# An attention kernel with top-1 experts: the row sum carried inside the probability tiles, one buffer of projection weights, and two router comparisons that read PSUM

## The chip, the cores and the metric

The kernel runs on one core of a Trainium2 chip. The metric is the device time of one execution in microseconds. Five engines work side by side, each through its own queue in order: TensorE (PE; PEld is its weight load), VectorE (DVE), ScalarE (ACT), GpSimd (POOL) and SyncE (SP), which here only issues DMAs. They wait for each other through semaphores. PE writes to PSUM, eight banks of 128 x 512 floats; DVE and ACT read it.

## The reference

Inputs are x of 4 x 2048 x 512 floats and the weights. The layer norm is without weights. Attention has 16 heads of 32, and filters queries and keys by a mask of their frequencies; the experts see the first 100 tokens that chose each of them.

```python
xn = layernorm(x)
q, k, v = split(xn @ w_qkv)                       # 16 heads of 32
q, k = spectral_filter(q), spectral_filter(k)     # rfft, times sigmoid(mask), irfft
attn = softmax(q @ k.T / sqrt(32))
y = (attn @ v) @ w_out + b_out

probs = softmax(xn @ w_gate)                      # 8 experts
best = argmax(probs)                              # the first one at equal values
# place of the token among those of its expert (cumsum); kept when it is below 100
expert = (dispatched @ w_expert + b_expert) * gate
x = x + y + expert
```

All of it is in float32.

## The kernel before

The work is cut into 16 **groups** k (four batches times four groups of four heads), each into four **blocks** n of 512 queries, each into eight **windows** w of two key tiles (128 keys each, one called even and one odd). There are 512 windows. Per tile and pair of heads u, PE adds a bias (the negative row maximum, negm, as three bf16 rows, `shift`) and the scores (`scores`) into two PSUM banks; ACT takes the exponential into a probability tile of 128 x 2 x 2 x 512 floats (8 KB per partition); one tile later PE multiplies it with the values (`products`), and DVE adds the result to `num` (ACT copies the first one into it).

The maxima of a later block are computed in the same windows: PE computes the scores once more the other way round (`max_matmuls`, array<-q,k and array<-k,q in the profile), DVE reduces them (`max_reduce`, part<-array). Two banks that lie side by side are reduced by one instruction, banks 7 and 0 by two (`joined`). `max_close` (line 468) turns the maxima of a block: PE transposes, ACT copies (rest<-array), POOL splits them into three bf16 rows (row<-rest), SP stores these to negm. It runs at the end of a block's seventh window (window 6), and the next block needs it with its first matmul.

**The row sum.** The softmax's denominator is the sum of all 16 tiles of a block. In the window after a pair, POOL issues a DMA that adds the odd tile to the even one (`pair`, line 823, even<-odd in the profile). One window later POOL adds this to the block's own tile `acc`, in two halves (`add_to`, line 826, acc<-acc,even). Tile 0 of a block is `acc` itself. Buffers: `acc` two, even three, odd two (lines 156 to 167). A buffer is free again when every reader of it is done.

**Closing a block.** `close_steps` (line 621) gives steps with a distance in windows from the block's end: `fold` (2) sums `acc` over the keys on PE and stores the sums (sums<-den), `fetch` (3) loads them spread over all partitions (few<-sums), `invert` (4) takes reciprocals on DVE and stores them (inverse<-few), `spread` (5) loads them as factor, `divide` (6) multiplies on POOL (ot<-num,factor), `result` (7, 7, 8, 8) projects a quarter each on PE and copies it to y on ACT, `add` (9) adds y to the output by a POOL DMA (out_dram<-y). The last block of all closes in `close_last` (line 666), with four tiles left to PE.

**Order.** Inside the main loop every compute instruction stays in the order of the program on its engine. The order between these works is an agenda, a list of steps for each window: half of a window's steps run after the even tile, half after the odd one. `plan` (line 774) fills it: the 12 projections of group k + 1 (`query_key`, `value`, with weights wg), the loading of weights (`load_qkv_weights`, line 374), in every third group of a batch the statistics and the bias of the next batch (x loaded to xs, POOL adds b_out, xs stored to the output), in every fourth its normalization, transposes and routing. SP's DMAs are placed by the scheduler, which may issue them earlier than the program says as long as their data are there. `place_experts` (line 756) puts the experts into the last groups.

**Routing** (lines 294 to 317) works on tiles of 128 x 16 x 8: the best probability per token (`best`), a comparison with it, a weight that falls with the expert's number (`ranked`), and a second comparison (`first_best`) which leaves one expert per token. Both comparisons are DVE instructions with two inputs in SBUF.

In the profile nearly all of this has line L82, the helper that keeps the order; it is told apart by tiles.

Of the kernel before, what the change touches and what calls it, by code (L numbers as in the profile page):

```python
# [101 lines left out]
def attention_and_top1_experts(ctx: ExitStack, tc: tile.TileContext, a: dict, out: bass.AP):  # L102
# [52 lines left out]
    chunks = ctx.enter_context(tc.tile_pool(name="chunks", bufs=2))  # L155
    probs_pool = ctx.enter_context(tc.tile_pool(name="probs", bufs=2))
    work = ctx.enter_context(tc.tile_pool(name="work", bufs=2))
# [6 lines left out]
    def probs(odd):  # L164

        name = "odd" if odd else "even"
        return probs_pool.tile([P, 2, 2, QB], F32, tag=name, name=name, bufs=2 if odd else 3)

# [43 lines left out]
    def token_stage(b):  # L212
# [81 lines left out]
        def wide(row):  # L294
            return row.unsqueeze(2).to_broadcast(full)


        def below_top():
# [9 lines left out]
        def best():  # L308
            on.vector.reduce_max(gate, probs, axis=AX.X)
            on.vector.tensor_tensor(chosen, probs, wide(gate), ALU.is_equal)  # L310

# [3 lines left out]
        def first_best():  # L315
            on.vector.reduce_max(first, chosen, axis=AX.X)
            on.vector.tensor_tensor(chosen, chosen, wide(first), ALU.is_equal)

# [55 lines left out]
    def load_qkv_weights(k):  # L374
        wg[k] = weights.tile([P, NR, 3, P], F32, name="wg")
        nc.sync.dma_start(out=wg[k], in_=wd[k % NG])
# [244 lines left out]
    def close_steps(k, n, num, acc):  # L621
# [29 lines left out]
        def divide():  # L651
            held["ot"] = work.tile([P, QB], F32, tag="ot", name="ot")
            on.gpsimd.tensor_tensor(held["ot"], num, held["factor"], ALU.mult)
# [8 lines left out]

        steps = [(2, fold), (3, fetch), (4, invert), (5, spread), (6, divide)]
        return steps + [(7, result, 0), (7, result, 1), (8, result, 2), (8, result, 3), (9, add)]

    def close_last(k, n, num, tiles, y):

        b = k // NG
        pf = row_sums(tiles)
        ot = work.tile([P, QB], F32, tag="ot", name="ot")  # L670
        den = work.tile([P, QB], F32, tag="den", name="den", bufs=1)
        for t in range(TQ):
            cols = slice(t * P, (t + 1) * P)
            on.vector.reciprocal(den[:, cols], pf[:, cols])
            on.gpsimd.tensor_tensor(ot[:, cols], num[:, cols], den[:, cols], ALU.mult)
        for t in range(TQ):
            on.vector.tensor_tensor(y[:, t, :], y[:, t, :], project(k, ot, t), ALU.add)
            if t % 2 == 1:
                nc.sync.dma_start(out=o[b, n, :, t - 1 : t + 1, :], in_=y[:, t - 1 : t + 1, :])
# [39 lines left out]
    for i, item in enumerate(stream[:MAX_AHEAD]):  # L719
# [14 lines left out]
        if i in closing:  # L734
            max_close(*closing[i])
    load_qkv_weights(1)

# [4 lines left out]
    def at(window, step, *args):  # L742
        agenda[window].append(lambda: step(*args))
# [12 lines left out]
    def place_experts(start):  # L756


        begin, fetch, measure, scale, expert = expert_steps()
        first = start + 18  # L760
        at(first, begin)
        for i in range(ST):
            at(first + 1 + i, fetch, i)
            at(first + 3 + i, measure, i)
        at(first + 11, scale)
        for i in range(ST + 2):
            at(first + 12 + i, expert, i)
        for i in range(ST):
            free = start + GW + i * NW + 10
            for step in (gather_row, add_row, scatter_row):  # L770
                at(free, step, i)
                free += 1

    def plan(k):
# [18 lines left out]
        if k + 2 < B * NG:  # L793
            at(start + GW // 2, load_qkv_weights, k + 2)
        first, last = len(first_projections) if k == 0 else 0, GW - 1
        if c == NG - 2 and b + 1 < B:
# [11 lines left out]
        elif c == NG - 1:  # L808
# [7 lines left out]
            for i in range(len(first_route)):  # L816
                at(start + 10 + i, follow_route, i)
            first, last = 10, GW
        steps = projections(k + 1)
# [5 lines left out]

    def add_to(acc, tile):
        for u in range(2):
            on.gpsimd.tensor_tensor(acc[:, u], acc[:, u], tile[:, u], ALU.add)

# [4 lines left out]
    for k in range(B * NG):  # L834
        plan(k)
        for n in range(NQ):
            num = work.tile([P, QB], F32, tag="num", name="num")
            acc = probs_pool.tile([P, 2, 2, QB], F32, tag="acc", name="acc")
            tiles = {0: acc}
            for w in range(NW):  # L840
# [7 lines left out]
                for j in (even, odd):  # L848
                    if j > 0:
                        tiles[j] = probs(j == odd)  # L850
                    for u in range(2):
# [22 lines left out]
                if not last or w < NW - 1:  # L874
                    pairs[window + 1] = tiles[even], tiles[odd]
                    if 0 < w and not (last and w == NW - 2):
                        adds[window + 2] = acc, tiles[even]
                if last and w == NW - 2:
# [3 lines left out]
            if not last:  # L882
                for after, *step in close_steps(k, n, num, acc):
                    at(window + after, *step)
    products(*left)
    for step in agenda[window]:
        step()
    close_last(k, n, num, [acc, *(tiles[j] for j in (NT - 4, NT - 2, NT - 1))], y)
    for steps in agenda[window + 1 :]:
# [35 lines left out]
```

## Time and profile before

| | |
|---|---|
| Median of 3 runs | 4593.77 us (4593.59 to 4596.07) |
| The profiled execution | 4593.43 us, its span 4591.6 us |
| Granted PE clock | 0.99 |
| Busy PE, DVE, ACT, POOL | 4422.1, 3121.1, 2592.4, 2998.8 us |
| POOL adds to the row sum (128 x 1024) | 892, 2541 ns each |
| Exponentials (128 x 512) | 4096, 603 ns each |
| DMAs that add odd to even | 511, 1024 KB, 7.9 us to landing (447 of them; 7.5 for the 64 into acc) |
| DMAs that add y to the output | 63, 1024 KB, 9.7 us to landing |
| wg loads | 16, 768 KB |
| DMA queue of POOL (q0) | 606.88 MB, 67.1% of the 16 DMA engines |

How to read it: *busy* is the time in which an engine had an instruction, as a share of the span. *Idle before* a group of instructions is the time that its engine stood still just in front of them, and the releaser is what ended it. The *chain* goes back from the last instruction, at each step to what released it or to the instruction before it on its engine, so its shares add up to the span. The *clock* is the share of full speed that PE was granted. Times in a timeline are us from the start of the span.

### The profile page before, as it was taken

Reading aid. Unit: us, or ns where it says so; the run is one execution under the profiler, and the core shown is the slowest. Engines: PE = TensorE matmul, PEld = TensorE weight load, DVE = VectorE, ACT = ScalarE, POOL = GpSimd, SP = SyncE. Lnnn points to the kernel's source line nnn. Section 1 sums busy time; section 2 is a strip of 40 time slices with the busy share of each in tenths; the row PEclk is TensorE's granted clock in tenths of the full one; section 3 lists DMA queues with packets and bytes.
Section 4 is the critical chain, followed back from the end, with each engine's and each line's share of the span. In section 5 each row is a group of like instructions: output and inputs, shape, how many; then the busy total and the mean of one; then the engine's idle time right before and its main releaser. Section 6 shows DMA issues by size and latency. Waiting matters only on the chain.

```text
span 4591.6 us, 106112 instructions
## 1 busy us (share of the span) xinstructions
PE 4422.1 (96%) x44438; PEld 1879.6 (41%) x44438; DVE 3121.1 (68%) x3605; ACT 2592.4 (56%) x4937; POOL 2998.8 (65%) x2081
## 2 busy tenths in 40 slices
PE   6999999999999999999999999999999999999997
PEld 3434343433434344344343434344444444434332
DVE  4667677775666777776567676777667776677772
ACT  3445555565555555557455555555655565555564
POOL 0458666765676667677477666667567774776766
PEclk9999999999999999999999999999999999999998
DMA  4567787786676877788667777878767775777787
GB/s 124 135 145 143 149 160 150 174 195 150 133 154 140 165 147 152 149 194 196 132 133 155 152 154 142 163 153 210 164 123 159 150 160 118 153 164 160 154 170 151
DMA packets 193233, 708.89 MB, mean 154 GB/s; under 512 B 47778, under 2 KB 54084, under 8 KB 127344
## 3 DMA queue, kind: packets, MB, share of 16 engines
q0 software_dynamic: 110576, 606.88, 67.1%
q1 hardware_dynamic: 77800, 91.56, 6.4%
q8 instruction: 348, 5.70, 0.5%
q10 hardware_dynamic: 4376, 3.67, 0.4%
q14 instruction: 133, 1.09, 0.1%
HBM read 77.09 MB, written 89.99 MB: 36 GB/s over the span
## 4 chain that ended last, share of the span: by engine, by line
PE 78%; DMA 10%; POOL 5%; issue 3%; ACT 2%; DVE 1%; SPq 0%; ACTq 0%; POOLq 0%; DVEq 0%
PE array L82 78%; DMA even<-odd 6%; POOL acc L82 4%; DMA inverse<-few 1%; DMA factor<-inverse 1%; ACT odd L82 1%; DMA sums<-den 1%; ACT even L82 1%; DVE part L82 1%; DMA negm<-row 0%; SPq L647 0%; POOL ot L82 0%; DMA wd<-in_L_attn_w_qkv_dram 0%; DMA few<-sums 0%; PE array L387 0%
## 5 line engine op out<-in xcount | busy, mean ns | idle before, releaser
L82 DVE TENSOR_REDUCE part<-array 128x2 f32<-128x1024 f32 (+1 forms) x2292 | 2433.2, 1106 | 1258.8 <-PE array L82 1247.0
L82 POOL TENSOR_TENSOR acc<-acc,even 128x1024 f32<-128x1024 f32 x892 | 2167.8, 2541 | 333.9 <-DMA even<-odd 332.7
L82 PE MATMUL array<-k,q 32*128 32x512 f32 x8192 | 2219.0, 622 | 10.7 <-issue 7.1
L82 PE MATMUL array<-q,k 32*128 32x512 f32 x8192 | 2051.9, 594 | 1.7 <-issue 1.7
L82 ACT ACTIVATE odd<-array 128x512 f32<-128x512 f32 x2048 | 1059.7, 603 | 485.9 <-issue 228.6
L82 ACT ACTIVATE even<-array 128x512 f32<-128x512 f32 x1792 | 931.9, 603 | 454.9 <-PE array L82 361.1
L82 POOL DMA_DIRECT2D even<-odd x447 | 412.4, 923 | 820.3 <-ACT odd L82 706.0
L82 PEld LDWEIGHTS array<-k,q 32*128 32x128 f32 x8192 | 808.7, 184 | 180.3 <-DVE num L82 71.6
L82 PE MATMUL array<-negm,ones_b 3*128 3x512 bf16 x4096 | 797.8, 382 | 25.0 <-DMA negm<-row 9.1
L82 PEld LDWEIGHTS array<-q,k 32*128 32x128 f32 x8192 | 751.5, 186 | 22.0 <-issue 13.3
L82 DVE TENSOR_TENSOR num<-num,array 128x512 f32<-128x512 f32 x960 | 651.6, 679 | 110.9 <-PE array L82 70.8
L82 PEld LDWEIGHTS <-ones_b 3*128 3x128 bf16 x4096 | 203.5, 92 | 914.4 <-issue 781.9
L82 PE MATMUL array<-odd,v 128*32 128x512 f32 x4096 | 548.0, 606 | 26.4 <-ACT even L82 25.8
L82 PE MATMUL array<-even,v 128*32 128x512 f32 x3584 | 483.5, 611 | 32.3 <-ACT odd L82 32.0
L82 PE MATMUL array<-xnT,wg 128*32 128x512 f32 x4032 | 464.0, 592 | 1.0 <-DVE part L82 1.0
L82 PE MATMUL array<-wo,ot 128*32 128x512 f32 x2048 | 259.0, 598 | 21.5 <-POOL ot L82 12.1
L82 PEld LDWEIGHTS array<-xnT,wg 128*32 128x32 f32 x4032 | 132.0, 110 | 303.1 <-issue 269.7
L82 PEld LDWEIGHTS array<-odd,v 128*32 128x32 f32 x4096 | 81.2, 108 | 421.2 <-ACT even L82 363.5
L82 PEld LDWEIGHTS array<-wg,xnT 128*32 128x32 f32 x8192 | 226.1, 110 | 39.5 <-issue 21.3
L82 PE MATMUL array<-wg,xnT 128*32 128x128 f32 x8192 | 235.8, 273 | 1.2 <-issue 1.2
L82 ACT COPY y<-array 128x512 f32<-128x512 f32 x252 | 147.7, 586 | 142.8 <-PE array L82 142.8
L82 PEld LDWEIGHTS array<-even,v 128*32 128x32 f32 x3584 | 71.2, 108 | 377.4 <-ACT odd L82 366.2
(144 smaller groups left out, 1715.3 us busy)
## 6 DMA issues: line engine op xcount, KB each, us to landing
even<-odd POOLq DMA_DIRECT2D x447, 1024.0 KB, 7.9
acc<-odd POOLq DMA_DIRECT2D x64, 1024.0 KB, 7.5
out_dram<-y POOLq DMA_DIRECT2D x63, 1024.0 KB, 9.7
xs<-in_L_attn_x_dram SPq DMA_DIRECT2D x31, 1024.0 KB
out_dram<-xs SPq DMA_DIRECT2D x16, 1024.0 KB
factor<-inverse SPq DMA_DIRECT2D x252, 64.0 KB
wg<-wd SPq DMA_DIRECT2D x16, 768.0 KB
wo<-in_L_attn_w_out_dram SPq DMA_DIRECT2D x16, 256.0 KB
```

The lines of the kernel that those rows point to most:

```text
L82: done = act(*args, **kwargs)
```

## The change

The block's own tile goes. Every key tile lies in an even or odd tile, and POOL adds the sum of the pair before to the pair's even tile, so the last even tile of a block holds the sum. There are five even and three odd buffers. wg has one buffer, and its load stands at a group's last window in the program (for group 1 after the first group's own projections); the projections of groups 0 and 3 of a batch shift by a window or two. `divide`, `result` and `add` of a block stand one window later each, and so do the experts' steps behind them; ot has one buffer. In the last close the sum of all pairs up to the sixth lies in tile NT - 6. In the router, ACT copies the operand of both comparisons into a PSUM bank, and DVE reads it there.

```diff
-        return probs_pool.tile([P, 2, 2, QB], F32, tag=name, name=name, bufs=2 if odd else 3)
+        return probs_pool.tile([P, 2, 2, QB], F32, tag=name, name=name, bufs=3 if odd else 5)
...
+        def in_array(of):
+
+            copy = bank()[:, 0 : NT * E].rearrange("p (i e) -> p i e", e=E)
+            on.scalar.copy(copy, of)
+            return copy
...
-            on.vector.tensor_tensor(chosen, probs, wide(gate), ALU.is_equal)
+            on.vector.tensor_tensor(chosen, in_array(probs), wide(gate), ALU.is_equal)
...
-            on.vector.tensor_tensor(chosen, chosen, wide(first), ALU.is_equal)
+            on.vector.tensor_tensor(chosen, in_array(chosen), wide(first), ALU.is_equal)
...
-        wg[k] = weights.tile([P, NR, 3, P], F32, name="wg")
+        wg[k] = weights.tile([P, NR, 3, P], F32, name="wg", bufs=1)
...
-            held["ot"] = work.tile([P, QB], F32, tag="ot", name="ot")
+            held["ot"] = work.tile([P, QB], F32, tag="ot", name="ot", bufs=1)
...
-        steps = [(2, fold), (3, fetch), (4, invert), (5, spread), (6, divide)]
-        return steps + [(7, result, 0), (7, result, 1), (8, result, 2), (8, result, 3), (9, add)]
+        steps = [(2, fold), (3, fetch), (4, invert), (5, spread), (7, divide)]
+        return steps + [(8, result, 0), (8, result, 1), (9, result, 2), (9, result, 3), (10, add)]
...
-    load_qkv_weights(1)
...
-            free = start + GW + i * NW + 10
+            free = start + GW + i * NW + 11
...
-            at(start + GW // 2, load_qkv_weights, k + 2)
-        first, last = len(first_projections) if k == 0 else 0, GW - 1
+            at(start + GW - 1, load_qkv_weights, k + 2)
+        if k == 0:
+            at(len(first_projections), load_qkv_weights, 1)
+        first, last = len(first_projections) + 2 if k == 0 else 0, GW - 1
...
-            first, last = 10, GW
+            first, last = 10, GW - 1
...
-    def add_to(acc, tile):
+    def add_to(tile, sum_before):
         for u in range(2):
-            on.gpsimd.tensor_tensor(acc[:, u], acc[:, u], tile[:, u], ALU.add)
+            on.gpsimd.tensor_tensor(tile[:, u], tile[:, u], sum_before[:, u], ALU.add)
...
-            acc = probs_pool.tile([P, 2, 2, QB], F32, tag="acc", name="acc")
-            tiles = {0: acc}
+            tiles = {}
...
-                    if j > 0:
-                        tiles[j] = probs(j == odd)
+                    tiles[j] = probs(j == odd)
...
-                        adds[window + 2] = acc, tiles[even]
+                        adds[window + 2] = tiles[even], tiles[even - WIN]
...
-                for after, *step in close_steps(k, n, num, acc):
+                for after, *step in close_steps(k, n, num, tiles[NT - WIN]):
...
-    close_last(k, n, num, [acc, *(tiles[j] for j in (NT - 4, NT - 2, NT - 1))], y)
+    close_last(k, n, num, [tiles[j] for j in (NT - 6, NT - 4, NT - 2, NT - 1)], y)
```

More of the change, by code (lines that the diff above doesn't have):

```diff
@@ L155, in attention_and_top1_experts @@
     chunks = ctx.enter_context(tc.tile_pool(name="chunks", bufs=2))
-    probs_pool = ctx.enter_context(tc.tile_pool(name="probs", bufs=2))
+    probs_pool = ctx.enter_context(tc.tile_pool(name="probs", bufs=3))
     work = ctx.enter_context(tc.tile_pool(name="work", bufs=2))
@@ L669, in close_last @@
         pf = row_sums(tiles)
-        ot = work.tile([P, QB], F32, tag="ot", name="ot")
+        ot = work.tile([P, QB], F32, tag="factor", name="ot", bufs=1)
         den = work.tile([P, QB], F32, tag="den", name="den", bufs=1)
```

## The prediction

> **What bounds the kernel now.** I read the page first. TensorE (PE) is busy nearly all the time, and PE is most of the chain that ended last; a tenth of the chain is DMA and a twentieth GpSimd (POOL).
>
> ```profile
> PE 4422.1 (96%) x44438; PEld 1879.6 (41%) x44438; DVE 3121.1 (68%) x3605; ACT 2592.4 (56%) x4937; POOL 2998.8 (65%) x2081
> ...
> PE 78%; DMA 10%; POOL 5%; issue 3%; ACT 2%; DVE 1%; SPq 0%; ACTq 0%; POOLq 0%; DVEq 0%
> ```
>
> A busy PE is not PE at its peak, so I looked for the loss in durations. I cut the span at the first bias matmul (array<-negm,ones_b) of each head group and asked for the stretches. Groups 1, 2, 4, 5, 6, 8, 9, 10, 12 and 14 do the same PE work (x2732 to x2736 matmul records). Shown are groups 6, 8, 14 and the last, 15 (columns: length, busy of PE, PEld, DVE, ACT, POOL, then PE clock, DMA share, GB/s).
>
> ```profile
> 1818.90:2099.60 280.70, 266.33 (x2732) 111.08 (x2728) 200.89 (x243) 158.02 (x300) 200.04 (x138) 0.99 0.82 178
> ...
> 2400.40:2663.70 263.30, 261.89 (x2732) 110.82 (x2728) 188.99 (x213) 154.38 (x296) 183.47 (x126) 1.00 0.76 152
> ...
> 4063.10:4325.60 262.50, 261.77 (x2732) 110.95 (x2728) 189.10 (x210) 154.38 (x296) 189.57 (x130) 1.00 0.78 157
> 4325.60:4591.60 266.00, 225.87 (x1890) 83.52 (x1886) 150.26 (x173) 147.84 (x286) 178.06 (x118) 0.94 0.80 162
> ```
>
> The reader is to see that equal work takes 262.5 in one group and 280.7 in another. Against group 14 the other nine lose 5.2, 18.3, 8.4, 1.7, 18.2, 0.8, 7.0, 12.3 and 3.5 us: 75.4 in all. The largest losses are where POOL and DMA have most to do (groups 2, 6 and 10, which load the next batch). Groups 3, 7, 11 and 13 have other PE work; against group 11, groups 3 and 7 lose 10.4 more.
>
> The list of waits names the causes (us in total, times, longest), and one passage of the chain in group 6 shows how a pair's DMA reaches PE:
>
> ```profile
> ACT even L82 <- POOL acc L82: 83.9, 45, 2.7
> ...
> POOL ot L82 <- DMA factor<-inverse: 64.4, 25, 4.7
> ...
> ACT odd L82 <- DMA even<-odd: 48.3, 17, 8.2
> ...
> PEld array L82 <- POOL ot L82: 25.3, 17, 3.0
> ```
> ```profile
> 1969.79 17.85 DMA even<-odd
> ...
> 1987.78 2.07 POOL acc L82
> ...
> 1990.10 2.36 POOL acc L82
> ...
> 1992.48 0.60 ACT even L82
> ```
>
> The pair's DMA lands after 17.85 us (median 7.9) because it stands behind the 1 MB output store that POOL issues just before it. POOL's add is late, the exponential finds no free even tile, and PE follows. In the built order of before, an even tile of windows 4 to 7 waits for the add in the window just before it; an odd tile waits for the pair's DMA two windows back.
>
> **The change, part by part.**
>
> *A. Running sum in the tiles, five even and three odd buffers.* The counts stay: 892 adds (2541 ns each), 511 pair DMAs. In the built order of after, an even tile waits for the add of two windows back, and an odd tile for the DMA three back: one more window each (6.3 us bare, 8.2 on average). The two slot waits are 132.2 us in 62 cases, of which 36.2 in 13 cases lie in group 15. An ACT gap with no such wait is also about 0.94 (378.4 us in 402 waits of even for PE), so groups 0 to 14 hold 96.0 - 49 x 0.94 = 50 real. The longest of these in groups 0 to 14 is 3.9 us, less than the 6.3 gained. What is late next is POOL itself: its work per window is 5.1 for two adds and 0.9 for an issue, about 6.6 with the small steps, under 8.2; in groups 2, 6 and 10 a bias add of 1.5 brings it to 8.1, so there the lag is carried on. I take **-45**; bounds 25 (half is only put off) and 50.
>
> *B. Division, results and output store one window later.* POOL's wait for the factor (64.4 us) loses its cause: its longest is 4.7, the window is longer. PE's waits for ot go with it: 15.4 of PEld and 6.7 of PE's own in groups 0 to 14, overlapping, and one 4.4 us loss in group 2 whose factor came late. I take **-15**; bounds 7 and 20. The division now comes right before the next but one block's copy into num, which reuses its buffer; the copy stands a whole window behind it, which hides the 1.3 us. Without that cover ACT would wait and PE with it.
>
> *C. Two comparisons read PSUM.* One comparison of the first batch is an accident of 13 us:
>
> ```profile
> 281.87 0.28 DVE L82 TENSOR_REDUCE gate<-probs 128x16 f32<-128x128 f32 x1
> 282.18 13.16 DVE L82 TENSOR_TENSOR chosen<-probs,gate 128x128 f32<-128x128 f32 x1
> 295.26 2.34 DVE L82 TENSOR_REDUCE part<-array 128x2 f32<-128x1024 f32 x2
> ```
>
> Its neighbours take 292 to 406 ns. It lasts exactly while POOL runs without a gap (adds and bias adds from 282.22 to 295.18). PE's window takes 22.5 us there, at a clock of 0.78, against 11.6 at 1.00 for a window with the same steps in group 1: 10.9 lost. Comparisons that read the array in PSUM (placed<-array,chosen) take 291 to 292 ns all four times, and no num<-num,array sum is stretched. So **-11**; bounds 0 (the new copy finds another obstacle) and 13. The eight new ACT copies (between 253 ns for 16x128 and 586 for 128x512) cost 2 to 5 us of an ACT that is busy 56%: nothing on the path. They shift the banks by one between the two comparisons, so 20 double reductions become two single ones, 20 x (2 x 683 - 1220) = 3 us of DVE: nothing either.
>
> The Trainium skill ("SBUF — State Buffer", section "SBUF: two separate sides") calls the port that VectorE with two SBUF inputs shares with GpSimd an exclusive lock, kept for one whole instruction. By that the wait would end after one POOL add, about 3 us, and C would be worth 3; the row shows it lasting over several POOL instructions, so the row decides.
>
> *D. One buffer of wg.* In the built order each load waits for the last projection that reads the old weights, in window 4 or 5 of a group's last block. Before, the loads of later weights stand at that same point:
>
> ```profile
> 1529.95 0.34 SPq L376 DMA_DIRECT2D wg<-wd  x1
> ```
> ```profile
> 41.76 4.21 DMA wg<-wd
> ```
>
> The next group begins at 1554.7, 24.8 us on; the one transfer whose length the chain shows took 4.21. **0**; without the cover it is 4.21 x 11 = 46 us.
>
> The Trainium skill ("Trainium Kernel Development and Optimization", section "Best Practices") tells one to double-buffer so that DMA lies beside compute, which speaks against D. By that rule D would cost those 46 us and the sum would be -16; here the 24.8 us speak for none.
>
> *E. What is new and late.* The output store moves from window 1 to window 2, so the pair of window 2 is now the one that lands 6.5 to 10 us late (14.4 to 17.9 against 7.9). Its add comes in window 4, and POOL must have caught up by the end of window 6, where it casts the row maxima (negm) which PE needs at the next block's first matmul. Into group 15, the copy of the maxima ended at 4316.94, the casts began at 4320.51 after the division, the last bias store was issued near 4323.0 and PE read it at 4325.61: about 1.5 to spare once it landed. Now: 3.6 earlier without the division in front, 2 less time as the two results (1.0 each) leave window 7, and 3.3 to 6.8 later (the late landing less 2 x 1.6 of catching up). That is between -0.2 and -3.7; I take 1.2 late at 12 group starts, as windows with more PE work follow elsewhere: **+14**; bounds 0 and 44. SP's order is otherwise kept: sums, few, inverse, factor, negm.
>
> *F. Group 15 and the end.* Its real slot waits are 36.2 - 13 x 0.94 = 24, but its last block hangs on POOL's chain of DMAs and adds whatever the buffers. I take -10. Against it two results and the last y store now follow the last block's close: the store, issued by 4577.98 before, needs two results (1.0 each), a copy (0.6) and 1.3 of issue after 4578.1, about 4 to 5 us later, and it ends the span. **-5** together; bounds -24 and +5.
>
> **Sum:** -45 - 15 - 11 + 0 + 14 - 5 = -62. The profiled run took 4593.43 us with a span of 4591.6, so 1.8 lie around it; 4593.4 - 62 = **4531**. The median of the runs, 4593.77, is the same within 0.4.
>
> **Rivals.** *All covers hold:* A 50, B 20, C 11, F 24 and nothing new: 105, 4488. Group 14 speaks for it (it nearly runs bare); the 16 DMA engines at 0.82 in group 6 speak against. *The wait is only moved:* the pair DMAs set the pace where it hurts, A is carried on to the next full slot, and only B and C less F's tail remain, 15 + 11 - 5 = 21: 4572. For it: POOL waits 339.0 us for those DMAs, and more buffers make none of them shorter. *Slower:* the maxima become late at every block. Freed of the slots, PE runs ahead of POOL, and the casts stand behind one more pair of adds, 5.1 us. Of 63 block starts I count some 16 with 1.5 us to spare, 32 with 4, the rest with 7: 16 x 3.6 + 32 x 1.1 = 93 us against a gain of 76 (A, B, C, F): 4610. It decides from 76 / 63 = 1.2 us per block. Against it: only 9.1 us of PE's waits are for negm now, and POOL has 1.6 us per window in hand. *Not what it says:* if the comparison still stalls, the time is 4542, inside the forecast.
>
> **Chances.** Forecast (4500 to 4565) 0.60, moved wait 0.15, all covers 0.10, slower 0.10, nothing left of it 0.05. A measurement of this kernel tells about 0.2%, 9 us, from no change. So faster 0.85, same 0.05, slower 0.10. The range runs from 4488 (A to F at their good ends) to 4580 (25 + 7 + 11 gained, 30 lost to E and F): it leaves out the slow rival and the unlikely end of the good one.
>
> **What would show it.** A: no long wait of ACT even for POOL or of ACT odd for the pairs' DMA, groups 2, 6 and 10 near 268. B: POOL ot no longer waiting for the factor. C: comparisons all under 0.5 us, the clock at 1.00 there. D: no wait for wg. E: PE or PEld waiting for negm at group starts, some 10 to 15 us. It is wrong if those waits stand at every block, if DVE waits for few (10.2 us now), or if group 6 still takes 280.

## The result, and the profile after

The changed kernel takes 4605.75 us (median of 20 runs, 4598.25 to 4621.58), the kernel before 4593.68 beside it (20 runs, 4581.18 to 4606.92). The ratio is 1.003 with an interval of 1.0021 to 1.004: 12 us slower in medians, where 62 us faster were forecast. The profiled execution took 4607.95 us, its span 4606.1, at a clock of 0.98.

The page after, busy time of the engines and the chain by engine:

```profile
PE 4435.0 (96%) x44438; PEld 1886.8 (41%) x44438; DVE 3102.1 (67%) x3625; ACT 2596.2 (56%) x4945; POOL 3001.0 (65%) x2081
...
PE 85%; DMA 7%; POOL 3%; issue 3%; ACT 1%; DVE 1%; SPq 0%; ACTq 0%; POOLq 0%; DVEq 0%
```

By this page the change worked: PE's share of the chain rose from 78% to 85%, those of DMA and POOL fell. Yet with the same 44438 matmuls PE is busy 12.9 us longer. A busy PE is not PE at its peak, so I went on to durations. Groups 6 and 15 (length, busy of PE, PEld, DVE, ACT, POOL, then PE clock, DMA share, GB/s):

```profile
1808.40:2085.90 277.50, 265.78 (x2735) 110.99 (x2732) 201.34 (x247) 157.95 (x300) 200.94 (x139) 0.99 0.82 179
...
4329.00:4606.10 277.10, 227.31 (x1905) 80.34 (x1902) 150.54 (x175) 149.29 (x288) 179.31 (x118) 0.91 0.76 155
```

Group 6 still takes 277.5 (268 was to be seen), and group 15 takes 11.1 longer, at a clock of 0.91 after 0.94. Over all groups, against the trace before: group 0 is 11.4 us shorter; groups 3, 7 and 11 are 9.0, 4.7 and 11.4 longer; group 15 is 11.1 longer; the other eleven are 10 shorter together. Group 6 holds the same matmuls as group 14, which takes 263.5.

Two waits that were small before (us in total, times, longest):

```profile
DVE few L82 <- DMA few<-sums: 10.2, 5, 5.7
...
PE array L82 <- DMA negm<-row: 9.1, 2, 5.0
```

The waits after, the rows that answer to those of before and the new ones:

```profile
DVE few L82 <- DMA few<-sums: 67.0, 13, 13.7
...
PEld array L82 <- POOL ot L82: 32.7, 15, 8.6
PE array L82 <- DMA negm<-row: 29.4, 5, 8.8
...
ACT even L82 <- POOL even L82: 4.1, 3, 2.0
...
ACT odd L82 <- DMA even<-odd: 2.4, 1, 2.4
```

The two slot waits of ACT are gone (132.2 us before, 6.5 now), and POOL's 64.4 us for the factor are gone altogether. In their place DVE waits 67.0 us for few (10.2 before), PE 29.4 for negm (9.1), and the results' wait for ot grew from 25.3 to 32.7.

**A long stall costs more than itself.** This is how few reaches PE, in window 4 of group 3's first block (timeline of DVE, then of PE; the bracket is the idle time before and what ended it):

```profile
1019.50 0.25 DVE L82 RECIPROCAL few<-few 128x16 f32<-128x16 f32 x1 [7.88 <-DMA few<-sums]
```
```profile
1013.79 0.66 PE L82 MATMUL array<-square,xs 128*128 128x128 f32 x4
1020.89 1.12 PE L82 MATMUL array<-square,xs 128*128 128x128 f32 x4 [6.44 <-DVE part L82]
```

DVE works in order. While its reciprocal waits for the DMA, no reduction of scores frees a PSUM bank, and PE stops for 6.44 us. Then look at the matmuls after it: 1.12 us for what took 0.66. The same stretch in slices of 1 us (the number after POOL's is the granted PE clock):

```profile
1018.00:1019.00 1.00, 0.00 (x0) 0.00 (x0) 0.00 (x0) 0.00 (x0) 1.00 (x1) 0.50 0.04 8
...
1024.00:1025.00 1.00, 1.00 (x14) 0.64 (x6) 0.88 (x1) 0.66 (x2) 0.58 (x1) 0.65 1.27 256
1025.00:1026.00 1.00, 1.00 (x14) 0.16 (x8) 0.88 (x2) 0.91 (x2) 0.00 (x0) 1.00 0.11 10
```

PE stopped at 1014.45. The clock falls to half 3.4 us later and comes back 3.8 us after PE went on, so by an estimate from these 3.8 us at half clock this stall of 6.44 cost some 1.9 more. That gave me the count that the prediction lacked, PE's idle gaps from the first bias matmul to PE's last matmul, from all PE records of each trace (time at half clock is counted to the end of the span):

| PE's idle gaps | before | changed | close_as_before | split_store |
|---|---|---|---|---|
| 0.3 to 3.3 us | 76, 87.9 us | 39, 44.6 us | 40, 46.3 us | 43, 49.9 us |
| longer | 5, 29.2 us | 10, 72.4 us | 8, 44.9 us | 5, 30.4 us |
| all | 118.8 us | 118.7 us | 92.6 us | 81.1 us |
| time at half clock | 75.6 us | 123.6 us | 105.7 us | 67.4 us |
| lost by it while busy | 27.0 us | 34.4 us | 38.3 us | 25.3 us |

(The last two columns are experiments that follow.) The change took away 43 us of short gaps, near the 45 that term A forecast, and put 43 us of long ones in their place. Of the 72.4 us of long gaps after, 36.8 end with DVE when few has landed (five gaps), 28.0 with the landing of negm (four), and 7.7 is a wait for ot in the last block. The span is 14.5 longer with the same idle time. The lower clock cost 7.4 more, but in compare_alone, which changes the router alone, it cost 35.3 us, 8.3 more than before: a difference of this size between two executions can't be put down to the change, and the rest of the 14.5 I can't assign.

### The profile page after: what moved, and what is told of

It is laid out like the page before. It is cut to its first block, busy times and chain, and to the rows that moved or that the text cites. A ratio compares the mean times of both kernels' runs of the same rounds, so it can differ in the third digit from the quotient of the medians.

```text
span 4606.1 us, 106228 instructions
## 1 busy us (share of the span) xinstructions
PE 4435.0 (96%) x44438; PEld 1886.8 (41%) x44438; DVE 3102.1 (67%) x3625; ACT 2596.2 (56%) x4945; POOL 3001.0 (65%) x2081
## 4 chain that ended last, share of the span: by engine, by line
PE 85%; DMA 7%; POOL 3%; issue 3%; ACT 1%; DVE 1%; SPq 0%; ACTq 0%; POOLq 0%; DVEq 0%
PE array L82 85%; DMA even<-odd 2%; POOL even L82 2%; DMA few<-sums 1%; DMA sums<-den 1%; DMA negm<-row 1%; DVE part L82 1%; ACT odd L82 1%; DMA wg<-wd 0%; POOL ot L82 0%; DMA wd<-in_L_attn_w_qkv_dram 0%; POOL table L82 0%; ACT even L82 0%; PE array L393 0%; POOL rest L82 0%
## 5 line engine op out<-in xcount | busy, mean ns | idle before, releaser
L82 POOL TENSOR_TENSOR even<-even 128x1024 f32<-128x1024 f32 x892 | 2179.2, 2568 | 218.9 <-DMA even<-odd 217.0
L82 ACT ACTIVATE even<-array 128x512 f32<-128x512 f32 x2048 | 1065.4, 601 | 506.0 <-PE array L82 484.6
L82 POOL DMA_DIRECT2D even<-odd x511 | 463.9, 908 | 1149.1 <-ACT odd L82 929.7
L82 PE MATMUL array<-negm,ones_b 3*128 3x512 bf16 x4096 | 800.9, 383 | 55.7 <-DMA negm<-row 29.4
L82 PE MATMUL array<-even,v 128*32 128x512 f32 x4096 | 549.5, 609 | 9.8 <-ACT odd L82 9.7
L82 PEld LDWEIGHTS array<-even,v 128*32 128x32 f32 x4096 | 80.9, 108 | 400.8 <-ACT odd L82 388.2
```

The source lines that it names most:

```text
L82: done = act(*args, **kwargs)
```

## The experiments

Theory 1: the closing steps one window later (terms B and E) cost the time, because the 1 MB store of y then goes out in window 2, beside the small DMAs of the sums, and takes their slack and the maxima's. The buffers (A) gain little besides, because the pairs that land late behind that store still hold POOL back in groups 2, 6 and 10. The rivals are named in each expectation. All were timed beside the kernel before; its median was 4590.65 us for the first four, then 4588.3, 4592.27 and 4594.01 for each four.

**store_back.**
```diff
-        return steps + [(8, result, 0), (8, result, 1), (9, result, 2), (9, result, 3), (10, add)]
+        return steps + [(8, result, 0), (8, result, 1), (9, result, 2), (9, result, 3), (9, add)]
```


> The changed kernel with the output store of a block (add) in window 1 again, as before; all else as changed. Theory 1, collision: the store, moved into window 2, stands in front of the block's fold in the list of steps (so the fold runs after the odd tile, 3.2 us later) and its 1 MB runs beside the small loads of sums and few, for which VectorE then waits (67.0 us against 10.2 before). Without it VectorE's wait for few falls under 20 us, the first blocks of groups 3, 7 and 11 lose their 6.6 us in window 4, and the time falls by some 35 us to about 4570. Theory 2, squeeze: tensor work arrives earlier since no slot makes it wait, and the reciprocal stands a fixed number of windows behind the fold; the store matters little, few keeps 50 us or more, and the time stays within 10 us of 4606. Theory 3, maxima: the bias rows are late at the starts of groups 3, 7, 11 and 15; neither this wait (29.4 us on TensorE) nor the time changes.

Measured: 4652.72 us, ratio 1.0123 (1.0106 to 1.014). The waits of this kernel:

```profile
POOL out_dram L82 <- ACT y L82: 188.9, 51, 11.8
...
PE array L82 <- DMA negm<-row: 66.7, 17, 15.4
```

DVE's wait for few is 19.4 us: few is in time again, so the diagnosis of few was right, and the forecast of the time wrong. Store and last results now share a window, and POOL's queue stands up to 11.8 us behind the results before it can issue the store. The maxima are late instead, in two ways: before groups 3, 7 and 11 their stores go out some 14 us ahead and land late (PE stops for 10.8, 13.4 and 15.4 us), at other starts, with stops of up to 5.2 us, POOL casts them late.

**close_as_before.**
```diff
-        steps = [(2, fold), (3, fetch), (4, invert), (5, spread), (7, divide)]
-        return steps + [(8, result, 0), (8, result, 1), (9, result, 2), (9, result, 3), (10, add)]
+        steps = [(2, fold), (3, fetch), (4, invert), (5, spread), (6, divide)]
+        return steps + [(7, result, 0), (7, result, 1), (8, result, 2), (8, result, 3), (9, add)]
...
-            free = start + GW + i * NW + 11
+            free = start + GW + i * NW + 10
```


> The changed kernel with all closing steps at the windows of before (divide 6, results 7 and 8, store 9; the experts' steps one earlier too): running sum in the tiles, eight buffers, one wg, comparisons on PSUM stay. Theory 1: the wait for few is back at 10 to 20 us; the division waits for the factor again (some 60 us of GpSimd, PE for ot some 10); time about 4575, a little over the store alone. Theory 2: few stays at 50 us or more and the factor's wait comes back on top: 4600 to 4620. Theory 3: the maxima stay late, 4600.

Measured: 4584.66 us, ratio 0.9976 (0.9963 to 0.9989), faster than both kernels; theory 1 had said about 4575. DVE waits 23.6 us for few, and POOL 58.3 for the factor again. The shift of the closing costs 21 us in medians, 25 in ratios. What is left for A, C and D is 6 us in medians, 11 in ratios. Why the buffers bring so little shows in one block, the third of group 6, before and here:

```profile
1953.60:2026.10 72.50, 67.84 (x882) 32.86 (x880) 53.12 (x68) 38.83 (x74) 55.65 (x40) 1.00 0.86 196
```
```profile
1939.80:2014.40 74.60, 70.05 (x881) 33.26 (x877) 52.95 (x68) 38.91 (x74) 56.65 (x41) 0.95 0.85 193
```

Before, PE lost the time in short waits, at a clock of 1.00. With deep buffers window 3 takes 7.7 us (10.4 before), then window 4 takes 16.2 (11.4 before), with one gap of 4.2, and the clock is 0.95 over the block. The chain there has the late pair, the add behind it, and the exponential that waited:

```profile
1956.20 17.62 DMA even<-odd
...
1976.26 2.34 POOL even L82
...
1978.62 0.60 ACT even L82
```

In the changed kernel itself the same window 4 takes 10.3 us. There the store goes out 1.2 us behind a pair and 6.8 ahead of the next one (2.0 before the next pair in the kernel before, by medians), and 5 pairs land more than 14 us after their issue, where 18 did before.

**reciprocal_later.**
```diff
-        steps = [(2, fold), (3, fetch), (4, invert), (5, spread), (7, divide)]
+        steps = [(2, fold), (3, fetch), (5, invert), (5, spread), (7, divide)]
```


> The changed kernel with the reciprocal of few (invert) one window later, at 5, with its store; the load of the factor follows in the same window. Theories 1 and 2 both: VectorE no longer waits for few (under 5 us), the time falls by 35 to 50 us, 4555 to 4570, less what the later factor costs the division (a few us of GpSimd waiting for it again). Theory 3: the time stays above 4595, since only the wait for few goes and the bias rows stay late at four group starts.

Measured: 4623.29 us, ratio 1.0059 (1.0042 to 1.0075). DVE's wait for few fell to 14.3 us, but PE's for negm rose to 72.7: SP issues inverse, factor and negm in this order, and a later inverse makes the maxima late.

**compare_alone** (the kernel before with the two comparisons reading PSUM, and nothing else).

> The kernel before with nothing but the two comparisons reading a PSUM copy. As the prediction has it, the one comparison of 13.16 us falls under 0.5 us and the time by 11 us, to about 4583 (0.2%). Rival: the copy on ScalarE or the banks shifted by one between the comparisons cost as much as they save, 4594.

Measured: 4589.98 us, ratio 0.999 (0.9977 to 1.0003). Group 0 fell from 313.6 to 304.2, but the profiled span is only 1.2 us shorter: the other groups are 8 us longer together (group 3 by 5.5), without a cause that I know. So the run neither shows nor excludes that the whole gains what group 0 gained. The comparison itself, in its row of the tile chosen (minimum, median, maximum in ns):

```profile
L82 DVE TENSOR_TENSOR chosen<-array,gate x1: 292/292/292, 282.9 to 282.9; 128x128 f32<-128x128 f32 x1
```

**closing_alone** (in the kernel before).
```diff
-        steps = [(2, fold), (3, fetch), (4, invert), (5, spread), (6, divide)]
-        return steps + [(7, result, 0), (7, result, 1), (8, result, 2), (8, result, 3), (9, add)]
+        steps = [(2, fold), (3, fetch), (4, invert), (5, spread), (7, divide)]
+        return steps + [(8, result, 0), (8, result, 1), (9, result, 2), (9, result, 3), (10, add)]
...
-            free = start + GW + i * NW + 10
+            free = start + GW + i * NW + 11
```


> The kernel before with only the closing steps moved: division, results and store one window later (7, 8, 8, 9, 9, 10). Theory 1 (the shift itself costs, because the 1 MB store then lies in window 2 beside the small DMAs of the sums and takes slack from few and from the maxima): DVE waits over 40 us for few, PE over 20 us for negm, and the time is 10 to 22 us over that of the kernel before, 4600 to 4613. Rival (the shift costs only together with the deep buffers, because PE then runs ahead of POOL): POOL's wait for the factor, 64 us, goes, and the time falls by the 7 to 20 us of term B, to 4572 to 4585.

Measured: 4612.14 us, ratio 1.005 (1.0032 to 1.0069): 24 us, a little above what theory 1 said. The shift costs as much without the deep buffers as with them. Its profiled execution was the fastest of seven (4591.93), so its waits (few 54.2 us, PE for negm 5.3) don't show the whole of it; the negm part of the expectation was not met.

**no_store** and **no_store_as_before**, the changed kernel and close_as_before without the stores of y.
```diff
-        return steps + [(8, result, 0), (8, result, 1), (9, result, 2), (9, result, 3), (10, add)]
+        return steps + [(8, result, 0), (8, result, 1), (9, result, 2), (9, result, 3)]
```


> The changed kernel without the stores that add y to the output (63 DMAs of 1 MB left out, so the attention's part of the output is missing). To be read beside the next run. Theory 1 (the store's place costs): DVE's wait for few falls from 67 us to under 20, the first blocks of groups 3, 7 and 11 fall from 73.5 to 66 or less, and the kernel is at most 6 us slower than the same kernel with the closing steps as before. Rival (the place of the division and the results costs: PE waits for ot at a block's first window): the ot waits of PE's weight loads stay near 32 us and the kernel stays 15 to 22 us slower than that one.

> The changed kernel with the closing steps as before (6, 7, 7, 8, 8, 9), without the stores that add y to the output. It is the other half of the pair: with the stores this pair stands 21 us apart. Theory 1: the gap closes to 6 us or less. Rival: it stays 15 to 22 us. The level of both tells how much the stores' traffic costs the buffers' gain: if the pair DMAs behind the stores are what holds POOL back in groups 2, 6 and 10, the wait of POOL for even<-odd falls from 392 us to under 250 and these groups from 280 to under 270.

The attention's part of the output is missing in both, except that of the last block. Measured: 4519.1 us (ratio 0.9847, 0.9821 to 0.9872) and 4514.58 (0.9851, 0.9832 to 0.987). The gap is 4.5 us in medians and none in ratios, to some 15 either way. So the shift costs through the store, and the first blocks of groups 3, 7 and 11 are back from some 73.5 us to 64 or less. few in the first of the two:

```profile
DVE few L82 <- DMA few<-sums: 1.8, 1, 1.8
```

PEld's waits for ot stayed at 38.8 us with the gap gone, so the rival fell. The level says more: 63 stores of 1 MB cost close_as_before 70 us in medians, 57 in ratios; 31 us of it lie in group 15. Without them POOL waits 236.0 us for its pairs (391.7 with them; under 250 was expected), and groups 6 and 10 take 268.5 and 266.4, the 268 that term A promised; group 2 takes 271.6, over the 270 that was expected.

**fold_first.**
```diff
                     at(window + after, *step)
+                if (k, n) > (0, 0):
+                    agenda[window + 2].insert(-1, agenda[window + 2].pop())
```


> The changed kernel with the sums (fold) ahead of the output store in the list of window 2, so that they run after the even tile again in blocks without projections there. Theory 1a (the 3.2 us that fold lost in the list are part of the lateness): DVE's wait for few falls from 67 us to 40 or less and the time by 4 to 10 us, to 4596 to 4602. Theory 1b (only the store's traffic beside the small DMAs delays few): the wait stays over 55 us and the time within 3 us, 4603 to 4609.

Measured: 4606.75 us, ratio 1.0033 (1.0019 to 1.0046); DVE waits 64.0 us for few. The sums left 3.2 us earlier in many blocks and few landed no earlier: it is the traffic beside it, not the place in the list.

**negm_first.** A load of wg or x is ordered behind the last stores of negm on SP's queue, and the next batch's first x load moves from a group's window 30 to 31.
```diff
+    def behind_maxima(load):
+        for one in stored[-3:]:
+            tc.add_manual_dep(load.ins, one.ins.name, ..., reason="behind the maxima")
...
-            nc.sync.dma_start(out=held[n], in_=x[b, n])
+            behind_maxima(nc.sync.dma_start(out=held[n], in_=x[b, n]))
...
-        nc.sync.dma_start(out=wg[k], in_=wd[k % NG])
+        behind_maxima(nc.sync.dma_start(out=wg[k], in_=wd[k % NG]))
...
-            at(start + GW - 2, in_stage, 0, 0)
+            at(start + GW - 1, in_stage, 0, 0)
```
What it is to undo is seen in SP's timeline of the changed kernel, before group 3 starts at 971.4, and in that of the kernel before, where it starts at 987.0:

```profile
950.50 2.08 SPq L382 DMA_DIRECT2D wg<-wd  x1
957.04 0.38 SPq L221 DMA_DIRECT2D xs<-in_L_attn_x_dram  x1
958.41 2.21 SPq L487 DMA_DIRECT2D negm<-row  x3
```
```profile
976.03 0.38 SPq L221 DMA_DIRECT2D xs<-in_L_attn_x_dram  x1
979.51 2.21 SPq L481 DMA_DIRECT2D negm<-row  x3
```

Three stores of 4 KB go out 1.4 us behind 1 MB, and their last one lands some 11 us later (in the chain 11.15, 9.14 and 12.13 us for groups 3, 7 and 11). POOL had cast these maxima within 2.0 to 2.9 us of ACT's copy. The order of SP was the same before (wg there at 971.00), with 3.5 us in place of 1.4 between x and negm; the last stores landed 5.2, 11.3 and 4.7 us after their issue, and of these three starts PE stopped at that of group 7 alone, for 5.0 us.

> The changed kernel, with the loads of wg and of x put behind the stores of the row maxima (negm) in the order of SP's queue. Theory 1 (of PE's 29.4 us of waits for negm, most are at the starts of groups 3, 7 and 11, because SP issues 768 KB and 1 MB just ahead of the three 4 KB stores): the wait falls to 10 us or less, these three starts lose at most 2 us each, and the time falls by 10 to 18 us, to 4588 to 4596. Rival (term E as forecast: POOL casts the maxima late, after the store in window 2): the waits stay over 20 us and the time within 4 us.

Measured: 4589.48 us, ratio 0.9994 (0.9981 to 1.0007), 16 us under the changed kernel, as theory 1 said. The waits:

```profile
ACT xs L82 <- DMA xs<-in_L_attn_x_dram: 17.0, 3, 6.8
...
PE array L82 <- DMA negm<-row: 4.6, 1, 4.6
```

PE's wait for negm is gone at these three starts, and part of it has become a wait of the normalization for x: groups 2, 6 and 10 are 26 us shorter together, groups 3, 7 and 11 are 16 longer.

**negm_first_as_before**, the same edit in close_as_before.

> The same order of SP's queue, in the changed kernel with the closing steps as before (4584.66 us in its own run, 18.8 us of PE waits for negm). Theory 1: the waits fall to 8 us or less and the time by 5 to 12 us, ratio to before 0.995 to 0.9965. Rival (the maxima are late through POOL's lag in groups 2, 6 and 10): no change, ratio 0.997 to 0.998.

Measured: 4593.02 us, ratio 1.0006 (0.9995 to 1.0017), slower than close_as_before. Neither theory said that. Its negm waits are gone too, but window 1 of groups 3, 7 and 11 takes 16.1, 16.3 and 12.5 us instead of 7.9, for x. The wait was moved with interest.

**split_store** (close_as_before with the store in halves).
```diff
-        def add():
-            on.gpsimd.dma_start(out=o[b, n], in_=held["y"], accum_op=ALU.add)
+        def add(half):
+            at = slice(2 * half, 2 * half + 2)
+            on.gpsimd.dma_start(out=o[b, n][:, at, :], in_=held["y"][:, at, :], accum_op=ALU.add)
...
-        return steps + [(7, result, 0), (7, result, 1), (8, result, 2), (8, result, 3), (9, add)]
+        return steps + [(7, result, 0), (7, result, 1), (8, add, 0), (8, result, 2), (8, result, 3), (9, add, 1)]
```


> The changed kernel with the closing steps as before, and the 1 MB store of y in two halves, one in window 0 and one in window 1 of the next block, so that a pair's DMA stands behind 512 KB at a time. Theory 1 (term A was lost because a pair that stands behind the store lands late and POOL, near its pace in groups 2, 6 and 10, carries the lag to the next full slot): the longest landings of pairs fall from 17 us to 13 or less, window 4 of the third block of groups 2, 6 and 10 falls from 16.3 to 12 us or less, and the time to 4565 to 4578. Rival (it is the stores' bytes, whatever their cut; POOL pays one more issue per block besides): within 6 us of 4585, or slower.

Measured: 4553.77 us, ratio 0.9905 (0.9888 to 0.9922), below the range of the expectation. Of 511 pairs, 4 land more than 14 us after their issue (16 in close_as_before), the longest after 15.0 (18.0; 13 was expected); window 4 of the three blocks takes 14.2, 10.3 and 11.1, where 12 was expected. In the table above the long gaps fall from 44.9 to 30.4 us; the short ones, 49.9 after 46.3, do not.

**store_w3** (the changed kernel with the store at 11, the experts' steps at 12).

> The changed kernel with the output store one more window later, in window 3 of the second next block (11 instead of 10). Theory 1 (each place of the store has its victim): few's DMA is through before it, so DVE's wait for few falls from 67 us to under 20; but the late pair is now that of window 3, whose add comes in window 5, and POOL has one window to catch up before it casts the maxima: PE's waits for negm rise from 29 to over 45 us, and the time stays within 10 us of 4606 or rises. Rival (only the small DMAs of the sums suffer from the store): with few free, the time falls to that of the closing steps as before, 4580 to 4592.

Measured: 4642.48 us, ratio 1.0104 (1.0086 to 1.0122). PE's wait for negm:

```profile
PE array L82 <- DMA negm<-row: 71.9, 17, 14.2
```

DVE's wait for few is 2.0 us. Each place of the whole store has its victim: the pairs behind it at 9 as before, few at 10, the maxima at 9 (with late results) and at 11. PE stops for 10.8, 10.5 and 14.2 us at groups 3, 7 and 11, where the stores of negm go out 14 to 15 us ahead: again half of the wait is at the starts with the loads in front. This much loss was more than theory 1 had said.

**split_before** (the kernel before with the store in halves, as in split_store).

> The kernel before with nothing but the store of y in two halves (windows 0 and 1 of the next block). The buffers' own worth is the distance to split_store (4553.77 us). Theory 1a (the store's late pairs took what the buffers give; without them the buffers bring 15 us or more): 4569 to 4585. Theory 1b (halving the store ends the very waits that the buffers should end, so the buffers bring nearly nothing in either form): 4550 to 4564, with ACT's waits of even for POOL and of odd for the pairs' DMA, 132.2 us before, under 60.

Measured: 4561.88 us, ratio 0.9941 (0.9921 to 0.9962). Slot waits of ACT here and in split_store:

```profile
ACT even L82 <- POOL acc L82: 44.6, 25, 2.7
...
ACT odd L82 <- DMA even<-odd: 22.8, 13, 4.0
```
```profile
ACT even L82 <- POOL even L82: 14.4, 7, 3.9
...
ACT odd L82 <- DMA even<-odd: 1.7, 2, 1.3
```

By the medians theory 1b holds (4550 to 4564): the smaller store ends half of the slot waits without any buffer. Buffers, comparisons and one wg together are then worth 8 us in medians and 17 in ratios, to 12 either way; the ACT waits, 67.4 us, are over the 60 of theory 1b. The interval doesn't part the two theories, but it excludes the 56 us of A and C.

**split_after** (the changed kernel with halves at 9 and 10).

> The changed kernel, its closing steps one window later, with the store of y in two halves (windows 1 and 2). Theory 1 (the shift costs because a 1 MB store lies beside the sums): DVE's wait for few falls from 67 us to 30 or less, and the distance to split_store falls from 21 to 10 us or less: 4556 to 4566. Rival (one half beside the sums is as bad): few stays over 50 us, and the time is 4570 to 4580.

Measured: 4567.31 us, ratio 0.995 (0.9935 to 0.9966). few fell to 36.7 us, between the two expectations; the distance to split_store is 13.5 us in medians, 20 in ratios to 11 either way. That the shift costs is confirmed; that halves make it cheaper is not.

**split_weights** (split_store with wg alone behind negm on SP's queue).

> split_store with the loads of wg behind the stores of negm on SP's queue, the loads of x where they are. In negm_first the maxima were in time, but the loads of x, put back too, made ACT's normalization wait 17 us. Theory 1: PE's waits for negm fall from 16 us to 8 or less and no normalization waits; the time falls by 4 to 10 us, to 4544 to 4550. Rival: the wait goes to another row, within 3 us of 4553.77.

Measured: 4555.41 us, ratio 0.992 (0.99 to 0.9939): the rival. PE's wait for negm fell from 16.0 to 4.1 us as theory 1 said, but POOL's for the pairs rose from 258.6 to 310.6 and PEld's for ot from 35.4 to 39.9.

**split_four** (split_store with four quarters, two in window 0, two in window 1).

> split_store with the store of y in four quarters, two in window 0 and two in window 1. If the size of each piece in front of a pair is what counts, the pairs land earlier still and the time falls by 3 to 10 us, to 4544 to 4551. If it is the number of issues on POOL (two more per block, some 1 us each, 126 us of POOL in all) or the bytes by window, which are the same, it is 4551 to 4565.

Measured: 4547.0 us, ratio 0.9903 (0.9883 to 0.9922), the best time here. By its median the size of a piece counts further; by its ratio it can't be told from split_store.

## Why the prediction was wrong

Two steps failed: in A the price of the slot waits, and in E the overlap of the store with the small DMAs, of which the sum has few at nothing and the loads in front of negm not at all.

**A: mechanism right, size wrong.** The slots are free, as forecast, but the term of 45 us (bounds 25 to 50) measured, together with D, 5 us with the closing as before (close_as_before less compare_alone in medians; 6 in ratios, to 8 either way). With the closing shifted A, C and D together are worth 6 us (the changed kernel less closing_alone in medians; 9 in ratios, to 10 either way). The step that failed is the price: "the longest of these in groups 0 to 14 is 3.9 us, less than the 6.3 gained", as if each wait were removed by itself. With the closing as before, POOL's lag is carried from window to window behind pairs that land late, so deeper buffers collect several short waits into one long one. Against compare_alone, which has C as well, close_as_before lost 45 us of short gaps and got 26 us of long ones (44.9 after 18.6); 12 of these 26 stand in that window 4 of groups 2, 6 and 10. That late pairs behind the store make this wait is shown by no_store_as_before, where window 4 takes 10.3 us in all three groups, and in two of the three by split_store. Yet with the store halved the buffers bring little too, since the smaller store ends half of the short waits by itself (split_before). In the changed kernel fewer pairs land late, and what the buffers freed went into the waits for few and negm of term E. What the trace before showed against me I had listed under the second rival: POOL waited 339.0 us for pairs that no buffer makes shorter.

**B: the wait of POOL went, the gain did not come.** POOL's 64.4 us are 0, but the results wait for ot as before: for the blocks of groups 0 to 14 PEld waits 14.2 us after 15.4, now in the next group's first window where it mostly was in the group's last. That the sum rose from 25.3 to 32.7 comes from the last close (8.6 after 3.0), and close_as_before has that wait too (8.4). I priced a wait of POOL as if PE stood behind it.

**C: right where it was read.** Forecast 11 (0 to 13); group 0 fell by 11.4 in the changed kernel and by 9.4 alone. In the time of the whole run it isn't shown: compare_alone gained 0.7 us in medians, 4.6 in ratios, to 6 either way. **D: nearly right.** One new wait came, 1.2 us of PE in group 0, where the load of group 1's wg took 15.0 us, not the 4.21 of the prediction's row; no other group waits for wg. No run undoes D alone.

**E: the step that turned the sign.** It took the store in window 2 for a matter of POOL and its casts alone, at 14 us, because "the pair of window 2 is now the one that lands 6.5 to 10 us late". Fewer pairs land late (5 after 18), and both victims were elsewhere. few I had put at nothing, and only named among what would show me wrong. And "SP's order is otherwise kept: sums, few, inverse, factor, negm" left out the loads of wg and x that SP puts in front of negm, in the trace before as well. PE's waits for negm rose by 20 us, near the 14 of the forecast, but that is luck: most of it stands at three starts and comes by another path, not at 12 starts by late casts. The chain of the changed kernel has both victims in it (start, length, here for groups 3 and 11):

```profile
1003.11 16.37 DMA few<-sums
...
3187.80 12.13 DMA negm<-row
...
3231.67 16.44 DMA few<-sums
```

The 8 KB of few take 16.4 us where a 1 MB store of POOL, a pair and a 1 MB load of x were issued within some 10 us before it (16.5 at group 7); in the kernel before they took 10.1 to 10.6 in these three blocks. B and E together, forecast at -1, measured +21 to +25. That the store is the cause is shown (no_store pair, and closing_alone for its independence of the buffers); that of the 29.4 us for negm the loads of wg and x on SP's queue are the larger part is shown by negm_first. Why the same loads delay negm more than before at groups 3 and 11 is not shown.

The Trainium skill ("DMA: Bandwidth & Descriptors", section "Issuing engines are not separate DMA queues") says that DMAs of all engines run on the same 16 DMA engines and interleave, whichever engine started them. The case agrees: SP's few goes from 10.1 to 16.4 us where the store that POOL issues is moved, and DVE waits 1.8 us for it without the stores.

**F: wrong sign.** Group 15 was to gain 5 us and lost 11.1. One wait for few, 13.65 us, stops PE for 12.54 in its second block. The tail is longer by 6.8 us (last window 42.3 after 35.5) where 4 to 5 were forecast; of that, 5.4 came already in close_as_before (40.9): PE's longest wait there is for ot. Whether PE merely arrives earlier is not shown; without the stores that tail is 33.7 us (no_store_as_before), so they have a part in it.

**The rivals.** The time came out near that of the slower rival (4610), but by luck, not by its mechanism: PE waited for the maxima at 5 starts, not at every block, and few, which that rival does not name, cost as much. "The wait is only moved" (4572) described A; what it lacked was that B would cost.

## What to carry to other kernels

Price a wait by what the engine that sets the end loses, and by its length: many short waits can be cheaper than the one long wait that deeper buffers make of them. Before a large transfer is moved, list the small ones that will be under way beside it and the in-order engines that wait for them, loads on the same queue included. If a large transfer has a victim wherever it stands, cut it: here halves alone gave 32 us in medians and 27 in ratios (split_before), while putting the whole one window later cost 21 us with the closing steps (close_as_before to the changed kernel) and another window for the store alone 37 more (store_w3), in medians.

## What the runs showed of the hardware

**The clock follows PE's gaps.** In the two traces, before and after, none of 33 gaps of 0.8 to 1.58 us at full clock was followed by half clock; of those from 1.59 to 2.7 some were (12 of 32); of those of 2.8 us and more all were (18). It came back 3.1 to 6.9 us after PE went on. The Trainium skill ("TensorE: Matmul & The Clock Gate", section "HAM oscillation — how this bites in real kernels") warns of gaps over about 3.4 us. All 15 gaps over 3.4 us agree; the rows also show that gaps of 1.6 to 2.7 us can be enough.

**Small DMAs beside large ones.** In the changed kernel negm's 4 KB land 1.6 us after the last issue at most starts and 9 to 12 at those where SP had just issued 768 KB and 1 MB (4.7 to 11.3 in the kernel before). few's 8 KB take from 1.6 to 16.5 us there.

**The same bytes in smaller pieces.** The store's landing went from 9.7 us for 1 MB to 6.8 for 512 KB (split_store) and 5.7 for 256 KB (split_four), and the pairs behind it gained: 16 (close_as_before), 4 and 2 of them land after more than 14 us. The place counts too: the 1 MB of the store take 12.5 us in closing_alone, one window later.
